# A state-space layer's gating moved from VectorE to GpSimd, and its skip term made one chunk later

## The chip, the core and the metric

The program runs on one core of a Trainium2 chip. A core has five engines that work side by side, each with an instruction list of its own that it runs in order: TensorE (PE in the profile, with its weight loads as PEld), VectorE (DVE), ScalarE (ACT), GpSimd (POOL) and SyncE (SP, which here issues DMA transfers). They wait for each other by semaphores. Data lies in SBUF (128 partitions); PE writes into PSUM, which in this kernel DVE and ACT read. The metric is the device time of one execution in microseconds (us); a comparison takes the median of several runs.

## The reference

The program is four layers; each adds an attention-like mixer and a feed-forward part, both fed by the same layer norm, to x of 4 sequences of 512 tokens and 256 channels, all in float32. The change is in the mixer of layer 0, a Mamba-2 block with 32 heads of 64 channels and a state of 128:

```python
proj = einsum('bld,pd->blp', xn, W_in)          # gate | xs, B, C | dt
hBC = silu(causal_conv(proj[..., INTER:INTER + CONV_DIM]))   # 4 taps
dt = softplus(dt + dt_bias); dA = exp(dt * -exp(A_log))
h = dA_t * h + (dt_t * x_t) B_t                 # step by step over 512 tokens
y_t = h C_t
y = y + D_param * xs                            # skip term
g = y * silu(gate)                              # gating
g = g * rsqrt(mean(g * g) + eps) * norm_w
out = einsum('bli,di->bld', g, W_out)
```

The other parts of the program (the gated feed-forward of layer 0 and the layers 1 to 3) are not touched.

## The kernel before

Layer 0 weaves two streams of work: the mixer (`mamba_pieces`) and the gated feed-forward (`glu_pieces`, L181 to L223). `weave` (L226) takes the next piece of whichever stream is less far along. What comes out is the order in which the program is written. At build time the framework then makes each engine's list from it: an instruction goes in when, by its own estimates, operands and buffers are ready, and among ready ones the one written earlier goes first. So a written order can be overtaken. `keep_in_program_order` holds an instruction behind the one that is written just before it on its engine. A tile with `bufs=2` has two buffers; the third use of it waits until the last reader of the first is done. Pool `m_t` has two buffers by default.

The mixer works through 4 sequences x 4 groups of 512 channels (8 heads), `i = 4b + g`, and in each group through 4 chunks `t` of 128 tokens, so 64 chunks. While a group's chunks are worked on, the next group's projections are made (`group`, L379: two projections of 128 x 512 per column group, ACT evicts the first as `cy` at L276, DVE adds three taps at L280, ACT applies silu at L284; the gate goes through silu at L400 into `sg`): two column groups beside chunk 0, one each beside chunks 1 and 2, none beside chunk 3. Between them and the chunks the feed-forward's matmuls lie (L134 for its projections, L212 for its down-projection, evicted by DVE at L158).

A chunk has these steps:

- `decays` (L403): SP brings the per-token decays into G (128 x 1024, three buffers), two chunks ahead.
- `before` (L413), one chunk ahead: DVE scans G along the tokens (L421); PE turns xs (L427); DVE scales it by dt into `xdt` (L429); ACT makes the skip term `xD` = D * xs in four instructions (L433); SP brings `eb`, the decays since the chunk's start (L437).
- `before_gpsimd` (L443): POOL multiplies G by C B (L447) and makes `xw` (L450) for the next chunk; it is written in the middle of `within`.
- `within` (L456): for t > 0, PE multiplies the state by C into `yb` (L468), DVE multiplies by `eb` into y (L469) and POOL adds xD (L470). PE updates the state (L476; DVE at L481 and L482, or ACT at L479 in chunk 0). PE multiplies xdt by G into `ya` (L486); DVE adds it to y, or to xD in chunk 0 (L491), and multiplies by `sg` (L492). ACT squares y (L494) and POOL sums the squares into `ssq` (L496, or L498 and L499).
- `project_out` (L502) of the chunk before: PE multiplies y by W_out (L507), DVE adds the result to `acc` (L513; ACT copies it for group 0 at L511). After a sequence's last chunk PE sums ssq over the channels (L518), and x gets its sum (L526).

PSUM tiles come from three rings: `mm` with four buffers (projections and state), `tr` with two (turned xs, L507, and the feed-forward's output) and `acc` with two (`ya` and `yb`). A tile whose reader is late holds up the PE instruction that wants its buffer.

The pins are on the matmuls of `ya` and on the addition L491.

Of the kernel before, what the change touches and what calls it, by code (L numbers as in the profile page):

```python
# [15 lines left out]
P = 128  # L16
# [66 lines left out]
def v3(ap, b):  # L83
    return ap.rearrange("p (a b) -> p a b", b=b)
# [161 lines left out]
def mamba_pieces(c, a, ws, open_pool):  # L246
# [4 lines left out]
    nc, tc = c.nc, c.tc  # L251
# [6 lines left out]
    dt_bias, a_log, norm_w, d_par = (  # L258
        ws[:, 666:698], ws[:, 698:730], ws[:, 730:746], ws[:, 746:762],
    )  # L260
# [27 lines left out]
    with tc.tile_pool(name="m_pre", bufs=1, side="right") as pool:  # L288
# [34 lines left out]
        for b in range(NB):  # L323
            pa, pc = c.ps("tr"), c.ps("acc")
            for t in range(TPB):
                cols = slice(t * P, (t + 1) * P)
# [20 lines left out]
    pb, pg2, pool = open_pool("m_b", 2), open_pool("m_g", 2), open_pool("m_t", 2)  # L347
    seqs, groups, chunks, w_in, Gs = {}, {}, {}, {}, {}
# [64 lines left out]
    def before(i, t):  # L413

        b, g = i // 4, i % 4
        CT, Btok, CB, acc, ssq = seqs[b]
        w, wo, xc, sg = groups[i]
        tt, hs, cols = b * TPB + t, slice(g * HG, (g + 1) * HG), slice(t * P, (t + 1) * P)
        G = Gs.pop((i, t))
        flat = G.rearrange("p h t -> p (h t)")  # L420
        nc.vector.tensor_tensor_scan(  # L421
            flat, flat, eye.rearrange("p h t -> p (h t)"), 0.0, ALU.mult, ALU.add
        )

        pt = c.ps("tr")
        for k in range(4):
            nc.tensor.transpose(pt[:, k * P : (k + 1) * P], xc[:, k, cols], c.ident)  # L427
        xdt = c.tile(pool, [P, 512], "xdt")
        nc.vector.tensor_mul(v3(xdt, HD), v3(pt, HD), by_head(dt[:, tt, hs]))  # L429
        eb = None  # L430
        xD = c.tile(pool, [P, 4, P], "xD")
        for k in range(4):
            nc.scalar.mul(xD[:, k, :], xc[:, k, cols], d_par[:, 4 * g + k : 4 * g + k + 1])  # L433
        if t > 0:
            eb = c.tile(pool, [P, 4, P], "eb")
            for half in range(2):
                nc.sync.dma_start(  # L437
                    eb[half * HD : (half + 1) * HD],
                    since[tt, g * HG + half : (g + 1) * HG : 2, :].partition_broadcast(HD),
                )  # L440
        chunks[i, t] = [G, xdt, None, xD, eb]

    def before_gpsimd(i, t):  # L443
        b, g = i // 4, i % 4
        chunk = chunks[i, t]
        G, xdt = chunk[:2]
        nc.gpsimd.tensor_mul(G, G, seqs[b][2][:, t, :][:, None, :].to_broadcast([P, HG, P]))  # L447
        if t < TPB - 1:
            chunk[2] = xw = c.tile(pool, [P, 512], "xw")
            nc.gpsimd.tensor_mul(  # L450
                v3(xw, HD), v3(xdt, HD), by_head(after[:, b * TPB + t, g * HG : (g + 1) * HG])
            )
# [3 lines left out]
    def within(i, t):  # L456

        b, g = i // 4, i % 4
        CT, Btok, CB, acc, ssq = seqs[b]
        G, xdt, xw, xD, eb = chunks.pop((i, t))  # L460
        tt, hs, cols = b * TPB + t, slice(g * HG, (g + 1) * HG), slice(t * P, (t + 1) * P)
        y = c.tile(pool, [P, 4, P], "y", bufs=3)
        if t > 0:
            S = state[i]
            yb = c.ps("acc")
            for k in range(4):
                ks = slice(k * P, (k + 1) * P)
                nc.tensor.matmul(yb[:, ks], lhsT=S[:, ks], rhs=CT[:, cols], start=True, stop=True)  # L468
            nc.vector.tensor_mul(y, v3(yb, P), eb)  # L469
            nc.gpsimd.tensor_add(y, y, xD)  # L470
        n = 4 * i + t + 1
        if n < 64:
            before_gpsimd(n // 4, n % 4)
        if t < TPB - 1:
            pst = c.ps()
            nc.tensor.matmul(pst, lhsT=Btok[:, t, :], rhs=xw, start=True, stop=True)  # L476
            if t == 0:
                S = state[i] = c.tile(pool, [P, 512], "S")
                nc.scalar.copy(S, pst)  # L479
            else:  # L480
                nc.vector.tensor_mul(v3(S, HD), v3(S, HD), by_head(etot[:, tt, hs]))  # L481
                nc.vector.tensor_add(S, pst, S)  # L482
        ya = c.ps("acc")
        for h in range(HG):
            part = slice(h % 2 * HD, (h % 2 + 1) * HD)
            mm = nc.tensor.matmul(  # L486
                ya[part, h // 2 * P : (h // 2 + 1) * P],
                lhsT=xdt[:, h * HD : (h + 1) * HD], rhs=G[:, h, :], start=True, stop=True,
            )
            tc.keep_in_program_order(mm)  # L490
        tc.keep_in_program_order(nc.vector.tensor_add(y, v3(ya, P), y if t > 0 else xD))  # L491
        nc.vector.tensor_mul(y, y, groups[i][3][:, :, cols])  # L492
        sq = c.tile(pool, [P, 4, P], "sq")
        nc.scalar.activation(sq, y, AF.Square)  # L494
        if g == 0:
            nc.gpsimd.tensor_add(ssq[:, t], sq[:, :2], sq[:, 2:])  # L496
        else:
            nc.gpsimd.tensor_add(ssq[:, t], ssq[:, t], sq[:, :2])  # L498
            nc.gpsimd.tensor_add(ssq[:, t], ssq[:, t], sq[:, 2:])  # L499
        return y  # L500
# [34 lines left out]
    decays(0, 0)  # L535
    decays(0, 1)
    before(0, 0)
    before_gpsimd(0, 0)
    behind = None
    for i in range(16):  # L540
        for t in range(TPB):
            if t == 1 and i % 4 == 3 and i < 15:
                yield from sequence(i // 4 + 1)
            taps = []
            for k in ((0, 1), (2,), (3,), ())[t] if i < 15 else ():
                taps.append(group(i + 1, k))
                yield 3.4
            n = 4 * i + t + 1
            if n < 63:
                decays((n + 1) // 4, (n + 1) % 4)  # L550
            if n < 64:
                before(n // 4, n % 4)
            yield 0.5
            for tap in taps:
                tap()
            y = within(i, t)
            yield 2.6
            if behind:
                project_out(*behind)
                yield 1.7  # L560
            behind = i, t, y
# [1246 lines left out]
```

## Time and profile before

| what | value |
|---|---|
| median of 3 runs | 3154.67 us (3148.51 to 3159.28) |
| profiled execution, its time | 3156.7 us |
| its span | 3154.9 us |
| PE busy | 3082.5 us (98%) |
| DVE busy | 1841.9 us (58%) |
| ACT busy | 1249.8 us (40%) |
| POOL busy | 627.9 us (20%) |
| granted PE clock, mean | 0.992 |
| layer 0's chunks | about 75 to 830 us of the span |

The profile is one execution, seen by the hardware. Busy time is that of an engine's own instructions; a busy share is a mean over all stages, so for a change in layer 0 the stretch from 75 to 830 us has to be looked at by itself. PE's matmuls overlap and their ends are modelled; a gap of PE that shows at all is a wait. In lists of waits the columns are engine and instruction, what ended the wait, and then total us, number of times, and the longest. In lists in order of time they are start, duration, engine, line, operation, output and inputs, form, and in brackets the idle time before with what ended it. Durations of POOL are rough.

### The profile page before, as it was taken

To read this page: it belongs to the slowest core of one execution; us is meant where nothing else is said; L and a number is where in the kernel's file an instruction comes from. 1 tells how busy PE (TensorE), PEld (TensorE's weight loads), DVE (VectorE), ACT (ScalarE), POOL (GpSimd) and SP (SyncE) were. 2 spreads that over 40 slices of the span, in tenths; PEclk is the share of its full clock that TensorE was granted. 3 is DMA by queue.
4 is the path that set the end of the run, shared out by engine and by line. 5 is a ranking of instruction groups with operands and counts; after the bars stand their busy time and mean duration, and the time that the engine had idled before them with its cause. 6 is when DMAs were issued, how large, how long until landed. Compare 5 with 4: busy or idle time off the path is not lost.

```text
span 3154.9 us, 35717 instructions
## 1 busy us (share of the span) xinstructions
PE 3082.5 (98%) x12502; PEld 1885.9 (60%) x12502; DVE 1841.9 (58%) x4656; ACT 1249.8 (40%) x2898; POOL 627.9 (20%) x521
## 2 busy tenths in 40 slices
PE   8999999999899999999999999999999999999999
PEld 5566566565655555555676656566566655555555
DVE  5778778777677787787666555554555522222222
ACT  4444435444356666666525333333333311111111
POOL 0465455555400123331223000000000000000000
PEclk9999999999899999999999999999999999999999
DMA  4233333332310234444233000000000000000000
GB/s 131 77 100 124 93 94 111 103 104 77 118 37 13 80 99 117 101 112 138 80 100 103 4 21 7 1 27 1 21 1 1 20 21 20 20 20 20 0 0 27
DMA packets 89090, 185.15 MB, mean 59 GB/s; under 512 B 14192, under 2 KB 57216, under 8 KB 84176
## 3 DMA queue, kind: packets, MB, share of 16 engines
q1 hardware_dynamic: 74448, 135.05, 13.4%
q0 software_dynamic: 14176, 47.01, 6.2%
q8 instruction: 99, 1.62, 0.2%
q10 hardware_dynamic: 288, 0.82, 0.1%
q14 instruction: 79, 0.65, 0.1%
HBM read 160.95 MB, written 12.98 MB: 55 GB/s over the span
## 4 chain that ended last, share of the span: by engine, by line
PE 79%; DVE 11%; DMA 5%; ACT 2%; POOL 2%; issue 2%; SPq 1%; DVEq 0%; ACTq 0%; POOLq 0%
PE mm L134 30%; PE acc L212 9%; PE mm L643 7%; PE mm L142 5%; PE acc L1116 4%; PE acc L659 4%; DMA G<-own 3%; DVE G L421 2%; PE tr L1108 2%; DVE cy L280 2%; PE tr L824 2%; PE tr L507 2%; PE acc L868 2%; PE mm L1446 1%; PE tr L212 1%
## 5 line engine op out<-in xcount | busy, mean ns | idle before, releaser
L134 PE MATMUL mm<-xnT,wu 128*128 128x512 f32 x2128 | 953.3, 595 | 4.2 <-DVE cy L280 2.0
L134 PEld LDWEIGHTS mm<-xnT,wu 128*128 128x128 f32 x2128 | 399.3, 191 | 468.7 <-issue 435.8
L650 ACT ACTIVATE pr<-pr,nm 128x128 f32<-128x128 f32 (+3 forms) x512 | 285.7, 558 | 306.9 <-DVE nm L646 304.5
L202 DVE TENSOR_TENSOR hT<-sg,mm 128x512 f32<-128x512 f32 x176 | 120.6, 685 | 386.3 <-PE mm L134 372.1
L201 ACT ACTIVATE sg<-mm 128x512 f32<-128x512 f32 x176 | 104.6, 594 | 591.5 <-PE mm L134 591.3
L646 DVE CUSTOM_DVE_ANT_0 pr<-mm,late 128x128 f32<-128x128 f32 (+3 forms) x512 | 245.4, 483 | 82.6 <-PE mm L643 80.9
L212 PE MATMUL acc<-wu,hT 128*128 128x256 f32 x1280 | 286.6, 380 | 0.3 <-DVE hT L167 0.3
L212 PEld LDWEIGHTS acc<-wu,hT 128*128 128x128 f32 x1280 | 241.7, 190 | 49.1 <-issue 17.7
L134 PE MATMUL mm<-xnT,w_in 128*128 128x512 f32 x512 | 230.8, 597 | 0.0
L986 POOL DMA_INDIRECT e<-in_p_experts,ids x128 | 128.4, 1003 | 454.1 <-DVE x L152 413.4
L421 DVE TENSOR_TENSOR_SCAN G<-G,eye 128x1024 f32<-128x1024 f32 x64 | 156.0, 2437 | 64.9 <-DMA G<-own 64.8
L447 POOL TENSOR_TENSOR G<-G,CB 128x1024 f32<-128x1024 f32 x64 | 151.5, 2368 | 172.3 <-DVE G L421 95.9
L643 PE MATMUL mm<-kf,qf 128*128 128x128 f32 (+3 forms) x512 | 177.2, 445 | 6.1 <-DVE qf L801 3.7
L280 DVE SCALAR_TENSOR_TENSOR cy<-mm,ws,cy 128x511 f32<-128x511 f32 (+2 forms) x216 | 158.6, 741 | 34.9 <-ACT cy L276 31.4
L643 PE MATMUL mm<-k,q 128*128 128x128 f32 (+3 forms) x512 | 176.5, 434 | 1.0 <-DVE q L1081 1.0
L134 PEld LDWEIGHTS mm<-xnT,w_in 128*128 128x128 f32 x512 | 97.5, 192 | 103.3 <-issue 97.2
L433 ACT ACTIVATE xD<-xc,ws 128x128 f32<-128x128 f32 x256 | 84.2, 391 | 180.6 <-POOL y L470 164.2
L152 DVE SCALAR_TENSOR_TENSOR x<-acc,cw,x 128x256 f32<-128x256 f32 x128 | 62.0, 484 | 153.6 <-PE acc L212 153.5
L1116 PE MATMUL acc<-PT,V 128*128 128x512 f32 (+3 forms) x512 | 149.1, 433 | 0.0
L1081 DVE TENSOR_SCALAR q<-mm,bias 128x512 f32<-128x512 f32 x64 | 48.0, 751 | 165.1 <-PE mm L134 165.1
L824 PEld LDWEIGHTS tr<-con,pr 128*128 128x128 f32 x640 | 79.4, 142 | 95.0 <-ACT pr L817 30.2
L507 PE MATMUL tr<-wo,y 128*128 128x256 f32 x512 | 126.5, 390 | 6.9 <-DVE x L158 3.8
(310 smaller groups left out, 4926.8 us busy)
## 6 DMA issues: line engine op xcount, KB each, us to landing
G<-own SPq DMA_DIRECT2D x64, 512.0 KB, 4.4
w_in<-in_m_units SPq DMA_DIRECT2D x16, 1024.0 KB, 5.1
eb<-since SPq DMA_DIRECT2D x96, 128.0 KB, 3.4
wu<-in_o_units SPq DMA_DIRECT2D x8, 1536.0 KB, 6.5
wo<-in_m_units SPq DMA_DIRECT2D x16, 512.0 KB, 4.1
psw<-pes SPq DMA_DIRECT2D x128, 64.0 KB, 2.8
wu<-in_g_units SPq DMA_DIRECT2D x4, 1536.0 KB, 6.8
wu<-in_f_units SPq DMA_DIRECT2D x4, 1536.0 KB, 7.3
```

Source lines behind the costliest of these rows:

```text
L134: c.nc.tensor.matmul(out, lhsT=w[:, d, cols], rhs=c.xnT[:, d, tokens], start=(d == 0), stop=(d == 1))
L142: c.nc.tensor.matmul(out, lhsT=c.xnT[:, d, tokens], rhs=w[:, d, cols], start=(d == 0), stop=(d == 1))
L212: nc.tensor.matmul(po[:, j, :], lhsT=hT[k][:, (t + j) * P : (t + j + 1) * P], rhs=wd[:, k, :], start=(i == 0), stop=(i == per - 1),)
L280: nc.vector.scalar_tensor_tensor(y[:, j:], src[:, : SEQ - j], conv[:, k, 3 - j : 4 - j], y[:, j:], ALU.mult, ALU.add,)
L421: nc.vector.tensor_tensor_scan(flat, flat, eye.rearrange("p h t -> p (h t)"), 0.0, ALU.mult, ALU.add)
L447: nc.gpsimd.tensor_mul(G, G, seqs[b][2][:, t, :][:, None, :].to_broadcast([P, HG, P]))
L507: nc.tensor.matmul(po, lhsT=y[:, k, :], rhs=groups[i][1][:, k, :], start=(k == 0), stop=(k == 3))
L643: nc.tensor.matmul(sc, lhsT=q[:, i * P : n], rhs=k[:, :n], start=True, stop=True)
L646: nc.vector.tensor_tensor_reduce(out=pr, in0=sc, in1=late[:, SEQ - n :], scale=1.0, scalar=-NEG, op0=ALU.add, op1=ALU.min, accum_out=nm,)
L650: nc.scalar.activation(pr, pr, AF.Exp, bias=nm, scale=-1.0, accum_out=total)
L824: nc.tensor.transpose(pt[:, (i - j) * P : (i - j + 1) * P], prs[s][i][:, j * P : (j + 1) * P], c.ident)
L1116: nc.tensor.matmul(z[:, j * P :], lhsT=head["V"][:, j, h, :], rhs=head["PT"][:, j, j * P :], start=(j == 0), stop=(j == TPB - 1),)
```

## The change

The skip term xD is no longer made in `before` of the chunk ahead, but in `within` of its own chunk, from the group's `xc`. In `within`, DVE adds `ya` to xD, in xD's own buffer, and does no more on it. For t > 0 POOL then adds y (the state's share, which DVE has multiplied by `eb` as before) to xD, one instruction as before, but after DVE's addition and no longer ahead of it. POOL multiplies by `sg` into y, in all 64 chunks; that was DVE's L492. xD's buffer is freed by this multiplication. Counts: DVE has 64 instructions less, POOL 64 more, ACT as many as before.

```diff
@@ before(i, t)
         eb = None
-        xD = c.tile(pool, [P, 4, P], "xD")
-        for k in range(4):
-            nc.scalar.mul(xD[:, k, :], xc[:, k, cols], d_par[:, 4 * g + k : 4 * g + k + 1])
         if t > 0:
             eb = c.tile(pool, [P, 4, P], "eb")
...
-        chunks[i, t] = [G, xdt, None, xD, eb]
+        chunks[i, t] = [G, xdt, None, eb]
@@ within(i, t)
-        G, xdt, xw, xD, eb = chunks.pop((i, t))
+        G, xdt, xw, eb = chunks.pop((i, t))
+        xc, sg = groups[i][2:]
         tt, hs, cols = b * TPB + t, slice(g * HG, (g + 1) * HG), slice(t * P, (t + 1) * P)
+        xD = c.tile(pool, [P, 4, P], "xD")
+        for k in range(4):
+            nc.scalar.mul(xD[:, k, :], xc[:, k, cols], d_par[:, 4 * g + k : 4 * g + k + 1])
         y = c.tile(pool, [P, 4, P], "y", bufs=3)
...
             nc.vector.tensor_mul(y, v3(yb, P), eb)
-            nc.gpsimd.tensor_add(y, y, xD)
...
-        tc.keep_in_program_order(nc.vector.tensor_add(y, v3(ya, P), y if t > 0 else xD))
-        nc.vector.tensor_mul(y, y, groups[i][3][:, :, cols])
+        tc.keep_in_program_order(nc.vector.tensor_add(xD, v3(ya, P), xD))
+        if t > 0:
+            nc.gpsimd.tensor_add(xD, y, xD)
+        nc.gpsimd.tensor_mul(y, xD, sg[:, :, cols])
         sq = c.tile(pool, [P, 4, P], "sq")
```

## The prediction

> **What bounds the kernel now.** First the page: is one engine full, and does it stay full in the part that changes?
>
> ```profile
> span 3154.9 us, 35717 instructions
> PE 3082.5 (98%) x12502; PEld 1885.9 (60%) x12502; DVE 1841.9 (58%) x4656; ACT 1249.8 (40%) x2898; POOL 627.9 (20%) x521
> ...
> PE   8999999999899999999999999999999999999999
> ```
>
> TensorE (PE) is busy 98% of the span. Layer 0's chunks run from about 75 to 830 us, the first ten or eleven slices, and there VectorE (DVE) is at 7 to 8 tenths. The table by stretches tells whether PE is full there too:
>
> ```profile
> 470.00:560.00 90.00, 90.00 (x441) 57.10 (x440) 73.06 (x101) 44.92 (x91) 50.25 (x33) 1.00 0.32 106
> 780.00:830.00 50.00, 38.91 (x241) 31.60 (x240) 35.54 (x52) 12.24 (x30) 28.14 (x23) 0.91 0.41 135
> ```
>
> Columns: stretch, length, busy PE, PEld, DVE, ACT, POOL, clock, DMA. In the middle PE is full although DVE is busy only 73 of 90 us; in the last 50 us it idles 11. So taking work from DVE pays only where PE waits for DVE. PE's own waits from 75 to 830 us (total, times, longest):
>
> ```profile
> PE tr L427 <- DVE x L158: 7.2, 2, 3.7
> PE tr L507 <- DVE x L158: 3.8, 2, 2.3
> ...
> PE tr L507 <- DVE acc L513: 2.7, 3, 1.0
> PE tr L368 <- ACT BT L284: 2.6, 2, 1.9
> ...
> PE mm L134 <- DVE cy L280: 2.0, 3, 1.2
> PE tr L121 <- DVE xdt L429: 1.0, 1, 1.0
> ```
>
> 16.7 us are put down to DVE, and 2.6 to ScalarE (ACT) behind DVE's taps. That is nearly all there is to win. The waits of the other engines over the chunks are much larger, but hidden under PE:
>
> ```profile
> ACT xD L433 <- POOL y L470: 164.2, 45, 9.0
> POOL ssq L498 <- ACT sq L494: 100.9, 48, 3.5
> DVE G L421 <- DMA G<-own: 64.8, 44, 2.9
> DVE y L491 <- POOL y L470: 42.2, 41, 3.6
> ```
>
> Last, the place where a chunk's y is wanted soonest: the third chunk of a group, whose successor follows 4.28 us later. Chunk 26 in order of time:
>
> ```profile
> 402.09 0.68 DVE L469 TENSOR_TENSOR y<-acc,eb 128x512 f32<-128x512 f32 x1
> 402.85 1.64 POOL L470 TENSOR_TENSOR y<-y,xD 128x512 f32<-128x512 f32 x1 [1.18 <-DVE y L469]
> 403.47 0.69 DVE L482 TENSOR_TENSOR S<-mm,S 128x512 f32<-128x512 f32 x1
> 404.53 0.69 DVE L491 TENSOR_TENSOR y<-acc,y 128x512 f32<-128x512 f32 x1 [0.36 <-POOL y L470]
> 405.25 0.69 DVE L492 TENSOR_TENSOR y<-y,sg 128x512 f32<-128x512 f32 x1
> 406.88 0.73 POOL L498 TENSOR_TENSOR ssq<-ssq,sq 128x256 f32<-128x256 f32 x1 [2.39 <-ACT sq L494]
> 408.06 2.50 DVE L421 TENSOR_TENSOR_SCAN G<-G,eye 128x1024 f32<-128x1024 f32 x1 [1.05 <-DMA G<-own]
> 410.70 2.36 POOL L447 TENSOR_TENSOR G<-G,CB 128x1024 f32<-128x1024 f32 x1 [2.29 <-DVE G L421]
> 410.93 1.99 PE L507 MATMUL tr<-wo,y 128*128 128x256 f32 x8 [1.03 <-DVE acc L513]
> ```
>
> y is done at 405.94 and used at 410.93: 4.99 us of slack. Read the same way, slack is 4.2 to 5.8 us at most third chunks, 1.33 at chunk 14, 5 to 16 at the other chunks, and 2.46, 0.90 and 0.05 at chunks 61 to 63.
>
> **The change, part by part.** *Gating leaves DVE*: 64 multiplications L492, 57.9 us in all, and the 42.2 us that DVE waits for GpSimd (POOL) at L491. The 100 us freed are mostly no gain: DVE's next instruction is often the scan L421, and it already waits 64.8 us for the transfer of G. The waits of PE at L158 and L513 show it: at 783.65, 694.4, 359.7, 408.1, 593.1 and 740.1 the scan ahead of the late eviction had waited 0.9 to 2.9 us for G, so those 3.5 + 3.8 + 2.7 us stay. Two parts can go. At 800.69 PE waits 3.7 us for an L158 behind the scan of chunk 63, itself behind a gating that took 2.43 us (799.50 to 801.93). Without it the scan starts at 799.5 or, if POOL's G of 799.03 to 801.38 holds it as it held the gating, ends by 803.5 (the longest scan, 4.03 us) instead of 804.13: 0.6 to 2.35, I take -1.5. The waits behind taps and xdt (2.0 + 1.0 + 2.6) may shrink: 0 to 5.6, I take half, -2.8.
>
> *Gating comes to POOL*: 64 times 1.26 us (the sum L470 at its shortest) to 1.65 (its median): 81 to 105 us on an engine busy 50 us of 90. Today POOL stands 2.2 us after each sum until DVE's two steps and ACT's square are through (128.5 us at L498 and L496); afterwards only about 0.8 us passes between the product's end and ssq (square 0.63, two hand-overs of 0.1). That gives back 64 x 1.4 = 90 us, so POOL's queue stays about as full as it is.
>
> *y comes later.* In chunk 26 the sum must now wait for ya as well: DVE's copy out of PSUM follows S at 404.16 and ends at 404.85; sum and product at 1.26 to 1.65 each end at 407.4 to 408.2, 1.4 to 2.2 us later than now, inside the 4.99. The other third chunks read alike: 0. Chunk 14, with 1.33 us, pays 0.1 to 0.9: +0.4. At the end no other work covers: following POOL's queue from chunk 61 (copy ends 810.8, sum and product 813.3, square, two ssq of 0.73 to 815.6, sum and product of 62 to 818.1, ssq to 820.4, sum and product of 63 to 822.9), the last projection starts at 823.0 instead of 822.34. With 1.65 per step it is 3.0 late; if POOL's order puts chunk 63's sum ahead of 62's ssq it is 0.8 early. I take +0.7, the shorter row being the one seen at 814.58 and 819.58.
>
> *The skip term* keeps its 256 ACT instructions (0.39 us) but is issued one chunk later, and its buffer, of two, is now freed by the product instead of the sum: 1.26 us later. ACT, in order, stands up to 9.0 us for that buffer, and behind it are queued the evictions of the next projections (cy L276, sg L400) that free PE's PSUM. This matters at the 16 last chunks of a group, where two column groups follow at once. At 417.31 the first eviction moved by 1.26 would end at 419.33, against taps that start at 419.23: 0.1. At 227.79 it hides entirely. At 371.36, where a layernorm has put a table load between, PE already waits 0.56 for sg: the full 1.26. Bounds: below, -1.3 (PE's waits for sg go, since a later-issued skip term may stand behind the evictions); above, 16 x 1.26 = 20.2. I take 13 x 0.1 + 3 x 1.26 = +5.1. DVE's add now also waits for xD; at today's lead (xD(28) is made at 404.5, used at 426.2) a shift of one chunk of 11.6 us stays covered, and if it were not, taps queued behind the add would be late too. SP's transfers of G and eb wait for PE's ya and DVE's L469, which do not move: 0.
>
> *Sum*: -1.5 - 2.8 + 0.4 + 0.7 + 5.1 = +1.9 on the profiled execution's 3156.7 us (span 3154.9 and 1.8 around it), which lies 2.0 above the median of the runs, 3154.67. Forecast: 3156.6.
>
> **Two rules beside the rows.** DVE's gating took 0.66 to 2.43 us, the long ones while POOL read SBUF (799.50 above). The Trainium skill, SBUF — State Buffer, "Who interferes with whom", says that a DVE instruction with two SBUF inputs and a GpSimd one that reads SBUF shut each other out entirely, whichever starts first. By it the 15 us of L492 above 0.664 each go, and POOL's product can be stuck behind a scan instead, as the sum at 176.39 was (3.25 us). By the rows the sum stands, since neither is on PE's path. Against the change speaks GPSIMD Engine Reference, "Engine selection": two-input elementwise work belongs on VectorE, GpSimd being about twice as slow. Were the product on the path, 64 x 1.26 would make 3235; the slacks say that it is not.
>
> **The rivals.** *Faster, PE no longer waits for DVE*: all 16.7 us go, 3138. For it: DVE is the engine PE waits for most. Against: ten of the 16.7 come behind G's transfer. *Slower, y late in the third chunks*: each engine's order is made anew when the kernel is built; if POOL gets G of two chunks on ahead of the product, y waits for that scan. In chunk 26: 413.06 + 1.26 = 414.3 against 410.93, 3.4 us; it decides once y is more than 4.99 us late. All 16: +54; half of them: +27, 3182. For it: POOL already takes G(29) ahead of chunk 27's sum. Against: G(29) lies 3.0 us behind ssq of chunk 26 today, and the product comes before its ssq. *Slower, ACT stands longer at xD*: the full 20.2, 3174.9. For it: the 164.2 us; against: at 227.79 it hides. *Nothing moves but waits* (DVE's time freed becomes waiting for G) is the forecast itself.
>
> **How the numbers follow.** A measurement of this kernel tells about 0.3% from no change, 9.5 us; the three runs shown spread over 0.34%. Forecast 0.46; faster 0.20; y late 0.20; ACT 0.14. So faster 0.20, same 0.46, slower 0.34. The range takes the faster rival's end, 3138, and the y-late rival at half the pairs, 3182; perhaps 0.05 lies below and 0.12 above. The forecast's own range is 3147 to 3165.
>
> **What would show it.** After: DVE busy about 58 us less, POOL 80 to 105 more; DVE's wait for POOL at the add gone and its wait for G grown; PE's waits at L158 and L513 behind scans still there; xD waiting on POOL's product. Wrong if PE shows waits for POOL's y of over 0.6 us per third chunk, or if PE's 16.7 us for DVE have gone.

## The result, and the profile after

The changed kernel is slower: 3194.25 us in the median (3188.51 to 3198.84) against 3154.67, a recorded ratio of 1.0115 with a 95% interval of 1.0099 to 1.0131 (the two medians divide to 1.0125, inside it). The forecast was 3156.6 and its range ended at 3182. The profiled execution took 3198.84 us, the slowest of the five. Two lines of its page:

```profile
span 3197.1 us, 35809 instructions
...
PE 3097.7 (97%) x12502; PEld 1893.3 (59%) x12502; DVE 1794.9 (56%) x4592; ACT 1241.7 (39%) x2898; POOL 746.7 (23%) x585
```

VectorE (DVE) has 47 us less to do: 57.9 us of gating are gone, and its scans take 11.4 us longer. GpSimd (POOL) has 119 us more: 86.7 are the gating, 32.7 sums of squares that got slower. The same 12502 matmuls are busy 15.2 us longer, and PE stands idle for 3197.1 - 3097.7 = 99.4 us instead of 72.4. Of the 42.2 us by which the span grew, 39.2 lie in layer 0: its last output projection ends at 863.5 us instead of 824.3, and what follows takes 2333.5 us instead of 2330.6. Of the 39.2 us, 26.3 are gaps of PE and 5.1 are granted clock that is missing (half speed for 23.9 us instead of 13.7); the other 7.8 us lie in matmuls that the records show as longer and are not split further. About 4 of the 39.2 us lie ahead of the first chunk's ya (108.5 us instead of 104.4), which starts at 101.6 to 108.5 in the kernels below, 3.9 us apart in two whose order up to there is the same. So some 35 us belong to the chunks.

The table by stretches, for the stretch in which PE was full before, and for the 5 us of it that are looked at below:

```profile
470.00:560.00 90.00, 82.64 (x390) 52.30 (x389) 60.45 (x81) 37.62 (x77) 55.63 (x35) 0.96 0.28 91
...
495.00:500.00 5.00, 2.63 (x10) 0.92 (x9) 2.25 (x3) 3.04 (x8) 3.76 (x3) 0.77 0.00 0
```

PE is no longer full, and neither DVE nor POOL is full either. PE's own waits over the chunks:

```profile
PE tr L509 <- DVE x L158: 7.8, 3, 3.7
PE mm L134 <- ACT sg L400: 7.8, 7, 2.2
PE mm L476 <- ACT sg L400: 7.2, 3, 2.5
PE tr L427 <- DVE x L158: 5.9, 2, 4.3
PE tr L121 <- DVE xdt L429: 5.7, 2, 2.9
PE tr L509 <- DVE acc L515: 3.4, 3, 1.5
```

New is ScalarE's (ACT's) eviction sg, 15.0 us where it had been about 1. The waits for DVE, which the change was expected to ease, went from 16.7 to 24.5 us (the five kinds that made the 16.7, with S L482 in place of cy). PE's wait for POOL's y is 0.9 us in one place. The waits of the other engines:

```profile
ACT sq L496 <- POOL y L494: 299.5, 64, 10.2
...
DVE G L421 <- DMA G<-own: 101.2, 49, 4.5
DVE cy L280 <- ACT cy L276: 75.7, 31, 7.7
...
POOL xD L493 <- DVE xD L491: 85.5, 31, 6.1
...
POOL ssq L500 <- ACT sq L496: 34.0, 46, 0.7
```

ACT stands for POOL in each of the 64 chunks, 299.5 us in all, at the square. Before, it stood 164.2 us for POOL at xD and 34.0 for DVE at the square. DVE in turn stands 75.7 us for ACT's eviction cy, which was 23.7. The two lines of before:

```profile
ACT sq L494 <- DVE y L492: 34.0, 41, 4.8
DVE cy L280 <- ACT cy L276: 23.7, 19, 3.1
```

Here is one such place of the changed kernel in order of time, the last chunk of a group and the first projections of the next:

```profile
487.25 2.62 DVE L421 TENSOR_TENSOR_SCAN G<-G,eye 128x1024 f32<-128x1024 f32 x1
487.69 4.34 POOL L444 TENSOR_TENSOR G<-G,CB 128x1024 f32<-128x1024 f32 x1
487.88 7.03 PE L134 MATMUL mm<-xnT,w_in 128*128 128x512 f32 x16
491.99 1.26 POOL L493 TENSOR_TENSOR xD<-y,xD 128x512 f32<-128x512 f32 x1
493.33 1.27 POOL L494 TENSOR_TENSOR y<-xD,sg 128x512 f32<-128x512 f32 x1
494.63 0.63 ACT L496 ACTIVATE sq<-y 128x512 f32<-128x512 f32 x1 [9.39 <-POOL y L494]
495.16 1.26 ACT L462 ACTIVATE xD<-xc,ws 128x128 f32<-128x128 f32 x4
496.33 0.76 ACT L276 ACTIVATE cy<-mm,ws 128x512 f32<-128x512 f32 x1
496.99 0.58 ACT L400 ACTIVATE sg<-mm 128x512 f32<-128x512 f32 x1
497.12 2.32 DVE L280 SCALAR_TENSOR_TENSOR cy<-mm,ws,cy 128x511 f32<-128x511 f32 x3 [6.93 <-ACT cy L276]
497.71 2.03 PE L476 MATMUL mm<-xw,Btok 128*128 128x512 f32 x2 [2.37 <-ACT sg L400]
```

And the same place before:

```profile
463.08 1.26 POOL L470 TENSOR_TENSOR y<-y,xD 128x512 f32<-128x512 f32 x1
464.38 1.28 ACT L433 ACTIVATE xD<-xc,ws 128x128 f32<-128x128 f32 x4 [5.85 <-POOL y L470]
465.04 7.03 PE L134 MATMUL mm<-xnT,w_in 128*128 128x512 f32 x16
467.26 0.63 ACT L494 ACTIVATE sq<-y 128x512 f32<-128x512 f32 x1 [1.12 <-DVE y L492]
467.80 0.76 ACT L276 ACTIVATE cy<-mm,ws 128x512 f32<-128x512 f32 x1
468.67 0.60 ACT L400 ACTIVATE sg<-mm 128x512 f32<-128x512 f32 x1
```

Before, the first eviction starts 2.76 us after the projection's first matmul; after, 8.45 us. ACT had nothing to do for 9.39 us and stood at the square, with the evictions queued behind it. PE fills its PSUM buffers and then waits 2.37 us.

### The profile page after: what moved, and what is told of

Read it like the earlier page. It is cut to its first block, busy times and chain, and to the rows that moved or that the text cites. A ratio compares the mean times of both kernels' runs of the same rounds, so it can differ in the third digit from the quotient of the medians.

```text
span 3197.1 us, 35809 instructions
## 1 busy us (share of the span) xinstructions
PE 3097.7 (97%) x12502; PEld 1893.3 (59%) x12502; DVE 1794.9 (56%) x4592; ACT 1241.7 (39%) x2898; POOL 746.7 (23%) x585
## 4 chain that ended last, share of the span: by engine, by line
PE 77%; DVE 8%; POOL 5%; ACT 3%; DMA 3%; issue 2%; SPq 1%; DVEq 0%; ACTq 0%; POOLq 0%
PE mm L134 29%; PE acc L212 9%; PE mm L645 8%; PE mm L142 5%; PE acc L1118 4%; PE acc L661 3%; PE tr L1110 2%; PE tr L826 2%; PE acc L870 2%; DMA G<-own 2%; DVE cy L280 2%; POOL xD L493 1%; PE acc L884 1%; PE mm L1448 1%; PE tr L509 1%
## 5 line engine op out<-in xcount | busy, mean ns | idle before, releaser
L212 PEld LDWEIGHTS acc<-wu,hT 128*128 128x128 f32 x1280 | 241.6, 190 | 49.4 <-issue 17.7
L421 DVE TENSOR_TENSOR_SCAN G<-G,eye 128x1024 f32<-128x1024 f32 x64 | 167.4, 2615 | 101.5 <-DMA G<-own 101.2
L280 DVE SCALAR_TENSOR_TENSOR cy<-mm,ws,cy 128x511 f32<-128x511 f32 (+2 forms) x216 | 158.9, 742 | 79.3 <-ACT cy L276 75.7
L444 POOL TENSOR_TENSOR G<-G,CB 128x1024 f32<-128x1024 f32 x64 | 159.1, 2486 | 100.7 <-ACT CB L373 78.9
L496 ACT ACTIVATE sq<-y 128x512 f32<-128x512 f32 x64 | 40.3, 630 | 299.5 <-POOL y L494 299.5
```

The costliest lines, as they stand in the source:

```text
L212: nc.tensor.matmul(po[:, j, :], lhsT=hT[k][:, (t + j) * P : (t + j + 1) * P], rhs=wd[:, k, :], start=(i == 0), stop=(i == per - 1),)
L280: nc.vector.scalar_tensor_tensor(y[:, j:], src[:, : SEQ - j], conv[:, k, 3 - j : 4 - j], y[:, j:], ALU.mult, ALU.add,)
L421: nc.vector.tensor_tensor_scan(flat, flat, eye.rearrange("p h t -> p (h t)"), 0.0, ALU.mult, ALU.add)
```

## The experiments

All ratios are to the kernel before on the same chip, with 95% intervals. The first eight runs were on chips where the kernel before takes 3161 us, the last ten where it takes 3227 to 3229; there the program behind layer 0 takes some 2400 us instead of 2331, at a lower granted clock. Layer 0 itself seems not to differ: in the run below whose ratio is 0.9999 it ends at 824.8. The times of layer 0 may therefore be read beside each other, with the care that each is one execution. The column "chunks" leaves out the start: it goes from the first ya to layer 0's end. The last columns are totals from 75 us to layer 0's end, in us: ACT standing for POOL, DVE standing for POOL, PE waiting for ACT's sg, PE waiting for DVE, and all gaps of PE.

| run | ratio | layer 0 ends | chunks | ACT<-POOL | DVE<-POOL | PE<-sg | PE<-DVE | PE idle |
|---|---|---|---|---|---|---|---|---|
| before | 1 | 824.3 | 719.9 | 164.2 | 42.2 | 1.3 | 17.1 | 23.1 |
| after | 1.0115 [1.0099, 1.0131] | 863.5 | 755.0 | 299.5 | 2.3 | 15.7 | 24.5 | 49.4 |
| e3_skip_late | 0.9996 [0.9984, 1.0009] | 829.1 | 725.1 | 162.3 | 39.7 | 0.5 | 21.0 | 27.0 |
| e2_gate_pool | 1.0049 [1.0031, 1.0067] | 841.2 | 739.6 | 254.4 | 54.3 | 1.4 | 26.1 | 38.6 |
| e1_gate_dve | 1.0051 [1.0035, 1.0067] | 842.1 | 740.2 | 0 | 86.0 | 0.4 | 22.2 | 35.4 |
| f6_fourth_as_before | 1.0059 [1.004, 1.0078] | 843.6 | 740.0 | 259.5 | 47.9 | 2.4 | 30.6 | 37.6 |
| f7_only_fourth | 1.0040 [1.0024, 1.0055] | 840.8 | 739.0 | 207.3 | 10.5 | 7.8 | 22.1 | 37.0 |
| e4_square_free | 1.0123 [1.0106, 1.0140] | 866.3 | 762.3 | 324.3 | 1.6 | 4.3 | 24.1 | 50.9 |
| e7_pool_order | 1.0131 [1.0114, 1.0148] | 877.5 | 770.8 | 306.1 | 11.4 | 13.4 | 31.7 | 55.2 |
| f3_square_later_xd3 | 1.0129 [1.0109, 1.015] | 875.0 | 767.5 | 304.1 | 4.4 | 9.1 | 22.8 | 55.4 |
| g1_scalar_pinned | 1.0034 [1.0019, 1.0048] | 841.6 | 733.5 | 92.5 | 0.3 | 5.5 | 13.5 | 34.8 |
| m1_pinned_last_now | 1.0030 [1.0018, 1.0042] | 837.9 | 733.7 | 100.9 | 0.7 | 5.1 | 18.8 | 35.5 |
| g4_before_xd_pinned | 1.0017 [1.0004, 1.0029] | 834.8 | 727.0 | 26.7 | 47.2 | 1.4 | 21.6 | 29.5 |
| m2_before_last_now | 0.9999 [0.9984, 1.0014] | 824.8 | 720.9 | 26.7 | 45.3 | 0.0 | 20.8 | 26.2 |
| h1_before_extra | 1.0042 [1.0026, 1.0059] | 836.6 | 734.8 | 185.2 | 55.0 | 0.6 | 27.7 | 34.9 |
| h2_extra_pinned | 1.0107 [1.009, 1.0124] | 859.0 | 751.5 | 58.7 | 64.9 | 2.6 | 29.4 | 47.5 |
| m3_extra_last_now | 1.0061 [1.0034, 1.0088] | 845.2 | 736.9 | 57.4 | 53.9 | 3.1 | 31.5 | 41.2 |
| k1_pinned_half_dve | 1.009 [1.0065, 1.0116] | 858.5 | 755.1 | 66.9 | 69.3 | 4.8 | 31.5 | 45.0 |
| k2_after_half_dve | 1.0213 [1.0196, 1.0231] | 892.1 | 790.5 | 302.5 | 142.5 | 12.7 | 50.0 | 71.8 |
| k3_before_half_dve | 1.0064 [1.0047, 1.0082] | 846.8 | 742.9 | 170.7 | 93.4 | 0.0 | 32.9 | 39.6 |

### The change in parts

The skip term alone, made beside its own chunk in the kernel before:

```diff
@@ before(i, t)
-        xD = c.tile(pool, [P, 4, P], "xD")
-        for k in range(4):
-            nc.scalar.mul(xD[:, k, :], xc[:, k, cols], d_par[...])
@@ within(i, t)
+        xD = c.tile(pool, [P, 4, P], "xD")
+        for k in range(4):
+            nc.scalar.mul(xD[:, k, :], xc[:, k, cols], d_par[...])
```

> Only the skip term moves beside its own chunk; sum and gating as before the change. Theory A: 3147 to 3163. Theory B: 3180 to 3195, with waits of VectorE or ScalarE at xD that grow. Theory C: 3147 to 3163.

0.9996: over ten executions no cost shows, though in the profiled one the chunks took 5.2 us longer. The gating alone, moved to POOL in the kernel before:

```diff
-        nc.vector.tensor_mul(y, y, groups[i][3][:, :, cols])
+        nc.gpsimd.tensor_mul(y, y, groups[i][3][:, :, cols])
```

> Only the gating goes to GpSimd; sum order and skip term as before the change. Theory A (ScalarE's square waits, in order, for GpSimd's late product, and the evictions of the projections stand behind it): the square's wait for POOL is over 200 us, PE waits for ACT's sg 8 us or more, time 3175 to 3195. Theory B (the skip term, issued a chunk later, holds ScalarE or VectorE up): 3147 to 3163, as before the change. Theory C (GpSimd has too much work, so that G itself comes late to PE): 3170 to 3190, with PE waits put down to POOL G or xw.

1.0049: a little under half the loss. The time lies in the ranges of theories A and C, but the signs of both are missing: the square stands only 86.0 us for POOL (xD 168.4), and PE waits 1.4 us for sg and not at all for POOL's G or xw. And the changed kernel with only its gating back on DVE, so that the sum after ya stays on POOL:

```diff
-        nc.gpsimd.tensor_mul(y, xD, sg[:, :, cols])
+        nc.vector.tensor_mul(y, xD, sg[:, :, cols])
```

> The changed kernel with the gating back on VectorE; GpSimd still adds the state's share, after VectorE's addition of ya. Theory A2: the sum stays behind G and xw in the fourth chunk and now VectorE, in order, waits for it as well, so little is won: 3175 to 3200. Theory D: GpSimd's added work is gone, 3150 to 3168.

1.0051: about the other half, and 3177.6 us lie in the range of theory A2 and not in that of D. ACT's square here stands 244.4 us for the product, which DVE makes, and DVE 86.0 for POOL's sum. Each step of POOL that comes to lie between ya and y costs about the same, and with only one of them there PE hardly waits for sg (0.4 and 1.4 us); by which way either half reaches PE was not tested. Next, by chunk: the changed kernel with the fourth chunk of each group summed and gated as before, and the complement.

```diff
+            if t == 3:                                   # f6; f7: if 0 < t < 3
+                nc.gpsimd.tensor_add(y, y, xD)
...
+        if t == 3:                                       # f6; f7: if t < 3
+            tc.keep_in_program_order(nc.vector.tensor_add(y, v3(ya, P), y))
+            nc.vector.tensor_mul(y, y, sg[:, :, cols])
```

> The changed kernel, but each group's fourth chunk is summed and gated as before the change (GpSimd adds the skip term early, VectorE adds ya and gates); the skip term stays beside its own chunk. Theory A2 (in the fourth chunk, 4.28 us behind the third, GpSimd's product stands behind the third's work, the next G and xw, ends 10 to 12 us after ya, and ScalarE in order behind it leaves PE's PSUM full): 3158 to 3175. Theory D (the loss comes from GpSimd's added work in all chunks alike): three quarters of it stay, 3183 to 3193.

> The mirror image: only each group's fourth chunk is summed and gated the new way, the first three as before the change; the skip term is beside its own chunk. Theory A2: 3180 to 3200, though GpSimd gets only 16 products more. Theory D: 3163 to 3175, a quarter of the loss.

The 16 fourth chunks alone cost 0.40%, the other 48 together 0.59%; the two add up to the whole within their intervals. A fourth chunk costs twice what another does, but the loss is not only there: both runs lie outside the ranges of theory A2, which put it there, and 3184.1 us with the fourth chunks as before fits theory D.

### Freeing ACT: two tries that did not free it

In the first, the square reads sg instead of y and so never waits for POOL.

```diff
-        nc.scalar.activation(sq, y, AF.Square)
+        nc.scalar.activation(sq, sg[:, :, cols], AF.Square)
```

> The changed kernel, but ScalarE squares the gate's silu, which is ready long before, in place of the gated y, so the square waits for no product of GpSimd; the norm is therefore of the wrong numbers. Work on every engine stays the same. Theory A: PE's waits for ACT sg fall from 15 us to under 3, time 3150 to 3168. Theories B and C: still 3183 or more, since neither the skip term nor GpSimd's load is touched.

Nothing was won (1.0123). The kernel leaves out the squares of y. The wait went one instruction further, to xD, whose buffer the same late product frees; PE's waits for sg fell from 15.7 to 4.3 us, but PE now waits 17.1 us for y itself:

```profile
ACT xD L462 <- POOL y L494: 292.4, 62, 8.9
...
PE tr L509 <- POOL y L494: 17.1, 8, 4.1
```

So freeing the square by itself wins nothing. In the second, the square was written with the next chunk's `project_out`, POOL's sums of squares behind it, and xD got three buffers, for which the state's tile gives up one of its two:

```diff
-        xD = c.tile(pool, [P, 4, P], "xD")
+        xD = c.tile(pool, [P, 4, P], "xD", bufs=3)
...
-                S = state[i] = c.tile(pool, [P, 512], "S")
+                S = state[i] = c.tile(pool, [P, 512], "S", bufs=1)
...
-        nc.scalar.activation(sq, y, AF.Square)           # in within
+        tc.keep_in_program_order(nc.scalar.activation(sq, y, AF.Square))   # in project_out
```

> The changed kernel with ScalarE set free of GpSimd's product on both counts: the square is written with the projection out of the next chunk and pinned there, and xD has three buffers (the state one, to make room). GpSimd's work is the same. If ScalarE is the way by which the late product reaches PE (A2): ScalarE's waits for POOL y fall from 299.5 us to under 120, PE's for ACT sg under 4, time 3155 to 3178. If the product reaches PE by another way: 3185 or more.

1.0129, but ACT had not been freed either. Its wait is only shared out anew, over xD and the square, 304.1 us in all:

```profile
ACT xD L462 <- POOL y L494: 162.9, 30, 10.9
ACT sq L501 <- POOL y L494: 141.2, 34, 8.3
```

This run says nothing on whether ACT's standing matters. Nor did an edit on POOL's side shorten the wait: G's product pinned behind what is written ahead of it on POOL.

```diff
-        nc.gpsimd.tensor_mul(G, G, ...)
+        tc.keep_in_program_order(nc.gpsimd.tensor_mul(G, G, ...))
```

> The changed kernel with GpSimd's product of G and CB pinned behind the instruction written before it, so it can no longer overtake the sum and product of the chunk before. Theory A: the square's wait for POOL falls from 299.5 us to under 180 and its longest from 10.2 to under 6, time 3155 to 3178. Theory B: 3185 or more. Theory C: 3185 or more, since GpSimd does the same work and G has less lead.

1.0131, with 306 us of standing. The pin kept G behind the sums of squares of the chunk before, but not behind this chunk's sum and product:

```profile
490.54 2.35 POOL L444 TENSOR_TENSOR G<-G,CB 128x1024 f32<-128x1024 f32 x1
492.85 3.02 POOL L449 TENSOR_TENSOR xw<-xdt,after 128x512 f32<-128x512 f32 x1
495.84 1.26 POOL L495 TENSOR_TENSOR xD<-y,xD 128x512 f32<-128x512 f32 x1
497.18 1.26 POOL L496 TENSOR_TENSOR y<-xD,sg 128x512 f32<-128x512 f32 x1
```

So it does not tell what G's place costs. In the changed kernel, of the 8.57 us from ya to y in a fourth chunk POOL spends 2.36 on the next chunk's G, 1.02 on xw and 1.80 on sums of squares, on the mean, and 3.18 on the sum and the product themselves.

### Freeing ACT: its order written out

Then both of ACT's instructions that wait for POOL were pinned: xD where it is written, behind the evictions, and the square with the next chunk's output projection, POOL's sums of squares behind it.

```diff
@@ within(i, t)
-            nc.scalar.mul(xD[:, k, :], xc[:, k, cols], d_par[...])
+            tc.keep_in_program_order(nc.scalar.mul(xD[:, k, :], xc[:, k, cols], d_par[...]))
...
-        nc.scalar.activation(sq, y, AF.Square)
@@ project_out(i, t, y)
+        tc.keep_in_program_order(nc.scalar.activation(sq, y, AF.Square))
```

> The changed kernel, with ScalarE's order written out: the square of a chunk is written with the next chunk's project-out, and the four skip-term products stay where the program puts them, behind the evictions cy and sg of the projections. Nothing on the other engines is edited. Theory C (ScalarE's channel: it stands some 280 to 300 us of layer 0 for GpSimd's late product in all the slow kernels, and the evictions behind it release TensorE late): ScalarE's waits for GpSimd's y (square and xD together) fall under 100 us, TensorE's waits for ScalarE's sg at lines of the state matmul and of the projection fall from 17.4 us under 4, VectorE's wait for ScalarE at cy (68.0) goes back to 20 to 35, TensorE's idle time in layer 0 goes from 49 to 35 or less, and the time is 3155 to 3178. Theory L (GpSimd's longer queue and its turns with VectorE's scan do it, whatever ScalarE does): ScalarE's waits fall as well, but TensorE's idle time stays at 45 or more and the time is 3188 or more. If ScalarE's wait for y stays over 200 us, the edit has not freed it and tells nothing.

1.0034: this is the first edit that gives most of the time back with all of POOL's added work left in place. ACT's standing for y (92.5 us) and PE's idle time (34.8) came out as theory C had it; PE's waits for sg (5.5) and DVE's for cy (38.9) fell less far. PE's and DVE's orders stay all but the same. POOL's does not, although none of its instructions is edited by itself: its sums of squares go with the square into `project_out`, and the next chunk's G is now often made ahead of them. No run tests POOL's new order by itself, but the traces show no way by which it gives time: y gets no earlier (below), PE's waits for POOL grow from 3.3 us to 10.8, DVE's were only 2.3 before the edit, and its scans take 2601 ns on the mean in place of 2615. And the run with three buffers for xD, whose sums went into `project_out` too, won nothing.

The edit may have a price at the ends of the sequences, where PE's sum over ssq wants the last square at once:

```profile
299.41 0.96 PE L522 MATMUL mm<-con,ssq 128*128 128x1 f32 x4 [2.68 <-POOL ssq L508]
```

So one more run, with the square of a sequence's last chunk (4 of 64) made at once, and the others as in the run before:

```diff
@@ within(i, t)
+        if i % 4 == 3 and t == TPB - 1:
+            squares(i, t, y, False)          # square and sums, not pinned
@@ project_out(i, t, y)
+        if i % 4 < 3 or t < TPB - 1:
+            squares(i, t, y, True)           # pinned
```

> The changed kernel with ScalarE's order written out as before (ratio 1.0034), but the square of the last chunk of a sequence (4 of 64) made at once instead of with the next chunk's project-out. If ScalarE's standing for GpSimd's late product carries the loss and the rest was the price of the edit (3 ends of a sequence, 6.2 us at the first), TensorE's wait for the sum of squares (3.9 us) goes, and the ratio is 0.999 to 1.002. If GpSimd's load carries the rest, the ratio stays at 1.003 to 1.005.

1.0030, at the upper of the two forecasts: the ends of the sequences had cost nothing that shows (the chunks take 733.7 us against 733.5; the 3.7 us by which layer 0 ends sooner lie ahead of the first ya), and the rest is something else. But of the change's 1.15 points, 0.85 are gone (0.65 to 1.05, with the two intervals' half-widths added in squares), 27 of 36 us; of the chunks in the profiled executions, 21.3 of 35.1 us. ACT's waits in this run:

```profile
ACT cy L276 <- PE mm L134: 122.4, 42, 7.4
...
ACT sq L455 <- POOL y L509: 66.6, 15, 13.3
ACT sg L400 <- POOL y L509: 34.3, 11, 5.0
```

ACT now waits for PE more than for POOL. And the end of a group:

```profile
179.94 7.03 PE L134 MATMUL mm<-xnT,w_in 128*128 128x512 f32 x16
181.78 0.39 DVE L527 TENSOR_TENSOR acc<-tr,acc 128x256 f32<-128x256 f32 x1
181.86 0.78 ACT L276 ACTIVATE cy<-mm,ws 128x512 f32<-128x512 f32 x1 [5.16 <-PE mm L134]
...
184.66 1.26 POOL L508 TENSOR_TENSOR xD<-y,xD 128x512 f32<-128x512 f32 x1
186.00 1.27 POOL L509 TENSOR_TENSOR y<-xD,sg 128x512 f32<-128x512 f32 x1
```

The eviction starts 1.92 us after the first matmul and ahead of y, not behind it. Measured over the first 11 fourth chunks, from the end of ya's matmuls: y is ready after 7.0 us before, 9.6 in the changed kernel, 10.3 here; the first eviction of the next group has ended after 8.5, 12.2 and 7.7; the next group's first ya starts after 15.3, 16.4 and 16.0. y is as late here as in the changed kernel. It is the evictions that are early again. That separates the lateness of y from what waits for it. The end of a group is one such place among several: of the 21.3 us, 4.7 come back between a fourth chunk's ya and the next, 10.7 between the first and the second chunk's, and 5.8 between the second and the third's, which also have the next group's projections beside them.

### The same order in the kernel before

> The kernel before, with the same order written out for ScalarE (square with the next chunk's project-out, skip-term products kept in place). Theory C: ScalarE stood 198 us for GpSimd there too and TensorE 16.7 us behind VectorE and 7 or so behind ScalarE; with the evictions ahead of the waiting instructions the time falls to 3140 to 3158. Theory L: nothing of GpSimd's queue changes, so 3155 to 3168 (no difference).

> The kernel before with ScalarE's order written out (ratio 1.0017 [1.0004, 1.0029]) and the square of the last chunk of a sequence made at once. If the standing at xD and at the square cost the kernel before something too, and the ends of the sequences hid it, the ratio is 0.995 to 0.999; if the standing of 198 us cost it nothing, 0.999 to 1.001.

The edits are those of the two runs above, on the kernel before. 1.0017 and 0.9999: ACT's standing falls from 164.2 to 26.7 us, and with the square of a sequence's last chunk made at once the time does not move. Before the change ACT stood a long time too, but that cost nothing that can be measured. No version of these runs beats the kernel before; the second of these and the skip term alone are level with it.

### POOL's load by itself

An idle product of the form of the gating, in the kernel before, read by nobody (the state's tile gives up one of its two buffers for the room):

```diff
-                S = state[i] = c.tile(pool, [P, 512], "S")
+                S = state[i] = c.tile(pool, [P, 512], "S", bufs=1)
...
+        extra = c.tile(pool, [P, 4, P], "extra", bufs=1)
+        nc.gpsimd.tensor_mul(extra, y, groups[i][3][:, :, cols])
```

> The kernel before, with one more GpSimd product for each chunk, of the form of the gating product, into a tile that nobody reads: 64 x 1.27 = 81 us more of GpSimd, none of it ahead of a y. Theory L (load and turns at the shared port): TensorE's idle time in layer 0 goes from 23 to 35 or more and the time to 3170 to 3185. Theory C: the product delays GpSimd's next G, xw and sum only where its queue is full, ScalarE's waits for GpSimd stay under 240 us, and the time is 3155 to 3168.

1.0042, 13 us for work whose result nothing waits for (14.9 us by the chunks): POOL's time is not free, even in an engine at 20%. The orders of PE, DVE and ACT are those of the kernel before, instruction for instruction, and ACT's copy into the state's single buffer (L479) waits 2.7 us in all, as before (2.8), and only for PE's matmul. So the buffer that was given up is not what costs. Then the same with ACT's order written out, first with the late square at a sequence's end, then without:

> The kernel before with the idle product of GpSimd for each chunk and, besides, ScalarE's order written out (the square with the next chunk's project-out, the skip-term products kept in place). The idle product alone had a ratio of 1.0042 [1.0026, 1.0059], the order alone 1.0017 [1.0004, 1.0029]. If GpSimd's load reaches TensorE through ScalarE's standing, ScalarE's waits for GpSimd's y fall from 185 us under 60, and the ratio is that of the order alone, 1.000 to 1.003. If the load costs without ScalarE (VectorE's scan, G, xw), the ratio is 1.005 to 1.008.

> The kernel before with the idle product on GpSimd and ScalarE's order written out (ratio 1.0107 [1.009, 1.0124]), the square of the last chunk of a sequence made at once. If the ends of the sequences carried the excess over the idle product alone (1.0042), the ratio falls to 1.001 to 1.005; if GpSimd's load costs TensorE time without ScalarE's standing (through VectorE, which stands for the product before its sum, 65 us there), it stays at 1.006 to 1.011.

1.0107, above both forecasts, and 1.0061, in the second. The idle product costs no less when ACT does not stand for POOL (57 us in place of 185), so its price does not go that way: by the chunks it is 14.9 us with ACT standing, and 16.0 without (736.9 against 720.9). What the trace shows in its place is VectorE. Of the run with the idle product alone, PE's waits and the scan (busy us, mean ns, then idle time before):

```profile
PE mm L134 <- DVE cy L280: 7.7, 7, 2.0
PE tr L427 <- DVE x L158: 6.8, 2, 4.0
PE tr L509 <- DVE acc L515: 5.8, 3, 2.6
```

```profile
L421 DVE TENSOR_TENSOR_SCAN G<-G,eye 128x1024 f32<-128x1024 f32 x61 | 162.1, 2658 | 54.8 <-DMA G<-own 52.6 <-POOL ssq L498 2.1
```

The scan's mean went from 2442 ns to 2658, DVE's standing for POOL's sum from 42.2 to 55.0, and PE's waits for DVE from 17.1 to 27.7. That DVE carries the price is read from these rows; no run tested it apart. Why the late square at the ends of the sequences costs 0.46 points here and next to nothing in the changed kernel stays open.

### Giving DVE a part of POOL's work

The second half of each chunk's sum of squares, from POOL to DVE, on three kernels (g1_scalar_pinned, after, before):

```diff
-            nc.gpsimd.tensor_add(ssq[:, t], ssq[:, t], sq[:, 2:])
+            nc.vector.tensor_add(ssq[:, t], ssq[:, t], sq[:, 2:])
```

> The changed kernel with ScalarE's order written out, and the second half of each chunk's sum of squares added by VectorE in place of GpSimd: 48 x 1.0 to 1.4 = 48 to 67 us off GpSimd, some 20 us on VectorE. Without the last edit the ratio was 1.0034 [1.0019, 1.0048]. If the rest of the loss is GpSimd's load, the ratio falls to 0.999 to 1.002 and GpSimd's product comes 1 to 2 us sooner; if it is the new order itself (ScalarE's or VectorE's), it stays at 1.003 to 1.005; above that VectorE's time is what is short.

> The changed kernel with the second half of each chunk's sum of squares on VectorE, ScalarE's order left to the planner. If the lateness of GpSimd's product comes from its queue, ScalarE's wait for y (299.5 us) falls by 48 x 1.0 or more, to 250 or less, and the ratio from 1.0115 to 1.005 to 1.009. If the lateness comes from the product's place behind ya's sum alone, the wait stays at 280 or more and the ratio at 1.010 to 1.013.

> The kernel before with the second half of each chunk's sum of squares on VectorE. If GpSimd is the engine that is short of time, ScalarE's wait for y at xD (164 us) falls, and the ratio is 0.996 to 1.000. If VectorE is (the change was made to free it), its 20 us more and the wait for the square behind ya's sum make TensorE's waits for VectorE grow over 16.7 us, and the ratio is 1.001 to 1.006.

All three are slower than their own starting point, by 0.56, 0.98 and 0.64 points. The second and third lie above the ranges that had been expected; the first lies where its expectation put the blame on DVE's time. ACT's wait in the changed kernel did not fall either (302.5 against 299.5). The new adds make DVE stand for POOL's first half:

```profile
DVE ssq L501 <- POOL ssq L500: 142.5, 47, 5.6
```

DVE's standing for POOL rises by 51 to 140 us, and PE's waits for DVE by 16 to 26. The 20 us of work and this standing come together here; which of them costs was not separated.

## Why the prediction was wrong

Four of its steps held. Making the skip term one chunk later costs nothing that shows by itself (0.9996). y came later by the 1.4 to 2.2 us that it gave: from the end of ya, the means by place in the group went from 2.42, 3.82, 3.26 and 6.60 us to 4.16, 5.96, 4.90 and 8.57, which is 1.7, 2.1, 1.6 and 2.0 more. The output projection's slack took that, as said: PE waits 0.9 us for y, and the rival with y late in the third chunks did not come. The end of the layer costs 1.4 us from the ya of chunk 60 on, against 0.7.

The step that failed is *The skip term*, which has ACT stand for xD's buffer, moves its release by 1.26 us, and counts that as 0.1 at most places, +5.1 in sum. The mechanism, ACT standing in order with the next projections' evictions behind it, was the right one; the instruction that stands and the size were not. The prediction asked only what a later freeing of xD does, and took y's lateness as a matter for the output projection. y has a second reader, ACT's square, which the build puts ahead of the next group's evictions at the place shown; and with product, square and xD tied together ACT waits for the end of POOL's whole tail. At the place shown, the evictions moved by 5.7 us against the projection, not by 1.26; over the first 11 fourth chunks by 3.7 on the mean. Taking two thirds of that standing away (299.5 to 100.9 us), with POOL's order changed beside it, brought back 27 of the 36 us (21.3 of 35.1 by the chunks); the term had a bound of 20.2. The rival *ACT stands longer at xD* named this way, but at 3174.9 us it was too small as well.

*Gating comes to POOL* failed in its conclusion. POOL got 119 us, not 81 to 105: the product itself took 86.7, but its sums of squares got slower too (L498 and L499 took 1116 and 938 ns before, L500 and L501 1348 and 1390 after). The time that it no longer stands for the square was right (128.5 us before, 41.4 after: 87, against 90). But the same edit made POOL stand 85.5 us for DVE's addition at L491, against 22.6 at L469 before, and the queue behind it did fill up: the time in which POOL stood for the scan's G fell from 95.9 to 14.9 us. What POOL's load costs without any of ACT's standing is a term that the sum did not have: 13 us for a like amount of idle work. The 0.30 points that are left in m1_pinned_last_now (13.8 us by the chunks) are of that order; that they are the same thing is not shown.

*Gating leaves DVE* was right that DVE's freed time turns into waiting for G (64.8 to 101.2) and that the waits behind scans stay. It was wrong in the -1.5 and -2.8, and DVE's busy time fell by 47 us, not by about 58, since the scans got longer. The 3.7 us wait in chunk 60 did go, 3.4 us were gained there, and chunk 61 lost 3.6. The waits of PE for DVE rose instead of falling (17.1 to 24.5 us), while DVE's taps stood 75.7 us for ACT's evictions in place of 23.7; with ACT's order written out that standing is 40.5 and PE's waits are 18.8.

Of the slacks, chunk 49's was 4.28 us and not 5 or more, which changes nothing in the sum. The statement on what would make the prediction wrong named two signs, waits of PE for y and the end of PE's waits for DVE. Neither came. The time was lost where no sign had been set.

## What to carry to other kernels

When an engine makes something later, list every reader of it, and for each reader what stands behind that reader in its own in-order list; the reader that empties PSUM counts most, even if it has slack to spare in the sum. A long wait of such an engine says little by itself: taking most of 164 us of standing away gained nothing in the kernel before, and taking 200 of 300 away gained 27 us in the changed one. What counts, as the places shown read, is whether the release comes before or after PE wants its buffers. Before work is moved to an engine because it is idle most of the time, put an idle instruction of the same form there for each and time it: here 64 of them cost 13 us.

## What the runs showed of the hardware

PE's clock is granted at half speed for 3.41 us, or a multiple, after PE has stood for shorter than that. In the place shown, PE stood 2.37 us, and the clock was 0.50 from 497.74 to 501.15. In each trace here the starts of all such stretches lie whole multiples of 3.413 us apart, so time can be cut into windows at these points. Over all kernels here, between 90 us and the end of layer 0, each of the 98 windows at full clock in which PE stood 1.98 us or more in sum was followed by half speed. Of the 4187 in which it stood less, 13 were followed by it, ten of them with 1.65 to 1.91 us. So a gap of 2 us counts by how it falls: of the 58 gaps of 2.0 to 2.8 us, 33 had a stretch begin between their start and 4 us after their end, and of the 46 above 3.4 us, 45. In the changed kernel the clock that was missing came to 11.9 us up to the end of layer 0, 5.1 more than before. The Trainium skill, TensorE: Matmul & The Clock Gate, Part 1, gives the half rate and a free-running window of about 3.4 us, which agree, and says that PE becomes slow after at least one idle window; here less than a whole window of standing was enough.

POOL and DVE shut each other out for whole instructions. POOL's product of G at 487.69, shown above, began beside a scan that ended at 489.87 and took 4.34 us: the 2.18 until then, and 2.16 more. Four of the 64 in that kernel began beside a scan and took 4.33 or 4.34 us; the other 60 took 2.35 to 2.38. The other way round, the scan at 487.25 began 0.48 us before POOL's xw ended and took 2.62 us: those 0.48, and 2.14 more.
